# Block sums on VectorE with one operand in PSUM, and an earlier outer sum for the last output blocks, in a feed-forward kernel of 49-product matrix algebra

## The chip, the core and the metric

The kernel runs on one core of one Trainium2 chip. A core has a matrix engine (TensorE, PE in the profile, with PEld for its weight loads), VectorE (DVE), ScalarE (ACT), GpSimd (POOL), a queue engine that issues transfers (SyncE, SP), and 16 DMA engines. SBUF is the working memory, PSUM the memory into which TensorE writes. The metric is the device time in microseconds (us) of one execution.

## The reference

```python
W = cond_weights[itok]                         # one 64x64 matrix for each of 32 batch rows
y = einsum('bct,bcd->bdt', x, W)               # x: 32 x 64 x 1024
h = gelu(y @ inter_w + inter_b)                # 1024 -> 4096, tanh approximation
out = x + h @ output_w + output_b              # 4096 -> 1024
```

All is float32. The 32 x 64 rows are 2048 rows of 1024 numbers for the two large products.

## The kernel before

Each of the two large products is computed by a scheme with 7 block products in place of 8, and it is applied twice, an outer level over quarters of the matrices and an inner level inside each quarter. So each stage has 7 x 7 = 49 products per group, and sums of blocks of the operands and of the results stand around them.

**Stage one** (`mm1`, L522, tiles `fA`, `fB`, `fC`) runs `nit` = 8 iterations of 49 products. Each product is 4 matmuls of 128x256, which the trace records as 8. `OUTER` gives the order of the seven outer products, `INNER` the order of the inner seven with the PSUM tag that each uses: A, B or C, two buffers for each tag. In every block of seven, B is used by one product alone (slot 1). An outer product that completes a quarter of the hidden layer ("fin" in `hidden`) has its result read out of PSUM by VectorE, passed through Gelu on ScalarE in place, combined into sums on VectorE, and stored to DRAM as an operand of stage two. In iterations 4 to 7 (`it >= NG`) `inner_s1` also adds the second half of each Gelu result to its first half, in SBUF, one add of 128x256 (`fD<-fD` and the like in the profile) for each of the four sub-blocks "11", "21", "22" and "12".

**Stage two** (`mm3`, L533, tiles `zA`, `zB`, `zC`) runs seven outer products `o`; each has seven blocks in the order `MID`, each block seven products of 4 matmuls (8 records). `read3` reads a product out of PSUM into tiles `mX`, `mY`, `mZ`, `mD`. `mid_z` adds X to Z after block 6. After blocks 2, 7 and 3, `outer3` combines the result with that of earlier outer products, adding the bias `b2` with one instruction per 128x256 half where an output is complete (`scalar_tensor_tensor`, L934). Outputs are complete in the outer products `o` = 1, 4, 5 and 6, eight tiles in each. A complete tile is transposed by TensorE into a PSUM tile of tag "B" (t = 0) or "C" (t = 1), `add_x` adds the loaded piece of x on VectorE, and `store_out` stores it. x comes through `load_xb` into a pool of 4 buffers (`xb`), issued on SP.

Operand sums are shared: large ones on GpSimd (`pool_add`, L181), others on VectorE (`add`, also L181), for which ScalarE often copies one operand to PSUM first (`to_psum`, L198, pool `pst` of two buffers; the add then shows as `hs<-h,t`, L181). The weights' outer sums for stage two are made in stage one from pieces `w2p`, and come back through DRAM as `v`.

The order is written by hand: each step is put at a time in slots of one product (`at(time, fn)`), the steps are sorted by time, and each engine executes its instructions in that order. `base + 7.35` in `hidden` is 7.35 slots after the start of the block that completes the quarter; the next block starts at `base + 7`. A slot lasts 1.73 us, the spacing of products in the trace.

## Time and profile before

| | |
|---|---|
| median of 3 timed runs | 1388.55 us (1385.87 to 1389.38) |
| the profiled execution | 1378.28 us, of which the span of the page is 1376.5 us |
| TensorE busy | 1343.7 us (98%) |
| VectorE busy | 964.7 us (70%), 1609 instructions |
| ScalarE busy | 423.5 us (31%), 834 instructions |
| GpSimd busy | 982.1 us (71%) |
| granted TensorE clock | 0.992 of full |

The table of windows shows the stages: from 0 to 34 us the mixing of x, from 34 to 734 us stage one with TensorE busy for 695.86 of 700 us, from 734 to 1370 us stage two with 616.48 of 636 us, and then 6.5 us of tail. Times of lines below are in us from the start of the span. In a group's row the figure after the bar is its busy time in us, then the mean duration of one in ns, then the idle time of the engine just before these instructions with what ended it. In a row of the timeline the figures are start and duration in us, the square bracket is idle time before it and what ended that. Rows of the timeline merge equal neighbours (x8), and their durations overlap by some 0.2 us on TensorE.

### The profile page before, as it was taken

How to read it: one execution, taken by the hardware profiler on the slowest of the kernel's cores; microseconds unless marked ns; L12 is line 12 of the kernel's file. 1: busy time of each engine (PE TensorE's matmuls, PEld its weight loads, DVE VectorE, ACT ScalarE, POOL GpSimd, SP SyncE). 2: the span in 40 equal slices, each digit the busy share in tenths (PEclk: the TensorE clock that was granted, in tenths of full speed). 3: DMA queues.
4: the chain of work that ended last, by engine and by line, in shares of the span. 5: the costliest groups of instructions: out<-in, count | busy, mean ns of one | idle time of the engine just before them, and what ended most of it. 6: DMA issues, size and time to landing. Idle time of an engine off the chain costs nothing. (4 is left out here: it accounts for less than half of the span.)

```text
span 1376.5 us, 18801 instructions
## 1 busy us (share of the span) xinstructions
PE 1343.7 (98%) x6568; PEld 1173.6 (85%) x6568; DVE 964.7 (70%) x1609; ACT 423.5 (31%) x834; POOL 982.1 (71%) x601
## 2 busy tenths in 40 slices
PE   9999999999999999999999999989999999999897
PEld 8888888888888888888888888878888888788786
DVE  3666565575786867668667666876767677798786
ACT  3424323243352422324214312313223222231130
POOL 7754757858677594884855949949689696694791
PEclk9999999999999999999999999999999999999999
DMA  8446675878897677577757072380631806618312
GB/s 286 148 156 216 206 244 212 268 248 287 288 322 256 236 231 242 201 241 248 270 176 265 17 292 82 130 329 8 223 144 46 336 16 255 220 46 324 119 39 69
DMA packets 134942, 273.39 MB, mean 199 GB/s; under 512 B 15424, under 2 KB 67648, under 8 KB 123200
## 3 DMA queue, kind: packets, MB, share of 16 engines
q1 hardware_dynamic: 134336, 271.66, 56.6%
q8 instruction: 53, 0.87, 0.2%
q0 software_dynamic: 512, 0.53, 0.1%
q14 instruction: 41, 0.34, 0.1%
HBM read 167.28 MB, written 104.86 MB: 198 GB/s over the span
## 5 line engine op out<-in xcount | busy, mean ns | idle before, releaser
L522 PE MATMUL fA<-yi,wi 128*128 128x256 f32 x896 | 213.8, 382 | 4.1 <-DVE fD L181 2.4
L533 PE MATMUL zA<-hs,wt 128*128 128x256 f32 x840 | 200.1, 382 | 5.1 <-DVE mD L181 3.1
L181 DVE TENSOR_TENSOR hs<-h,t 128x512 f32<-128x512 f32 x308 | 199.4, 676 | 6.7 <-POOL h L181 3.5
L181 POOL TENSOR_TENSOR h<-h,h 128x1024 f32<-128x1024 f32 x84 | 203.2, 2446 | 0.0
L522 PEld LDWEIGHTS fA<-yi,wi 128*128 128x128 f32 x896 | 169.6, 190 | 31.2 <-DVE fX L181 2.8
L533 PEld LDWEIGHTS zA<-hs,wt 128*128 128x128 f32 x840 | 159.2, 192 | 28.7 <-POOL h L181 2.6
L198 ACT COPY t<-hs 128x512 f32<-128x512 f32 x112 | 66.1, 590 | 223.4 <-DVE hs L181 223.3
L181 POOL TENSOR_TENSOR wi<-w 128x512 f32<-128x512 f32 x80 | 102.9, 1286 | 29.7 <-PE fC L522 24.0
L181 POOL TENSOR_TENSOR ws<-w,w 128x1024 f32<-128x1024 f32 x32 | 76.2, 2402 | 66.8 <-PE fA L522 57.0
L547 ACT ACTIVATE fD<-fD,b 128x256 f32<-128x256 f32 x128 | 57.8, 500 | 190.3 <-DVE fD L181 190.3
L198 ACT COPY t<-h 128x512 f32<-128x512 f32 x140 | 81.3, 592 | 88.1 <-DVE hs L181 85.2
L181 DVE TENSOR_TENSOR fX<-fA,fX 128x512 f32<-128x512 f32 x104 | 71.2, 684 | 42.9 <-PE fA L522 42.5
L181 POOL TENSOR_TENSOR wt<-v 128x512 f32<-128x512 f32 x35 | 45.3, 1296 | 74.0 <-DMA v<-w_d 72.4
L181 POOL TENSOR_TENSOR wi<-w,wi 128x512 f32<-128x512 f32 x40 | 50.8, 1271 | 61.7 <-PE fA L522 54.8
L522 PE MATMUL fC<-y,wi 128*128 128x256 f32 x384 | 91.0, 380 | 0.1
L522 PEld LDWEIGHTS fC<-y,wi 128*128 128x128 f32 x384 | 72.7, 190 | 10.3 <-issue 0.5
L533 PE MATMUL zC<-hs,v 128*128 128x256 f32 x336 | 79.5, 379 | 1.3 <-ACT mX L907 1.3
L181 POOL TENSOR_TENSOR wt<-v,wt 128x512 f32<-128x512 f32 x35 | 46.4, 1326 | 46.6 <-PE zA L533 46.6
L533 PE MATMUL zA<-h,wt 128*128 128x256 f32 x336 | 79.4, 379 | 0.0
L522 PE MATMUL fA<-yi,w 128*128 128x256 f32 x320 | 75.6, 379 | 0.0
L533 PEld LDWEIGHTS zC<-hs,v 128*128 128x128 f32 x336 | 63.8, 190 | 10.3 <-ACT mX L907 1.7
L533 PEld LDWEIGHTS zA<-h,wt 128*128 128x128 f32 x336 | 63.8, 190 | 8.6
(171 smaller groups left out, 2836.7 us busy)
## 6 DMA issues: line engine op xcount, KB each, us to landing
h<-hs_d SPq DMA_DIRECT2D x56, 1024.0 KB, 6.6
w<-in_L_ffn_inter_w_dram SPq DMA_DIRECT2D x32, 1024.0 KB, 6.2
hs_d<-hs SPq DMA_DIRECT2D x96, 256.0 KB, 3.1
v<-w_d SPq DMA_DIRECT2D x21, 1024.0 KB, 9.7
hs_d<-fD SPq DMA_DIRECT2D x64, 256.0 KB, 3.4
w2p<-in_L_ffn_output_w_dram SPq DMA_DIRECT2D x32, 512.0 KB, 5.0
w_d<-w2p SPq DMA_DIRECT2D x64, 256.0 KB, 2.9
w_d<-w2t SPq DMA_DIRECT2D x48, 256.0 KB, 6.6
```

Source lines behind the costliest of these rows:

```text
L181: eng.tensor_tensor(o, a, b, ALU.subtract if sub else ALU.add)
L198: nc.scalar.copy(t, src)
L522: nc.tensor.matmul(acc[:, u, :], lt[:, k, ts(u, P)], rt[:, k, :], start=start and u == 0 and k == 0, stop=k == 1, skip_group_check=True,)
L533: nc.tensor.matmul(acc, wl[:, k, :], hr[:, k, :], start=start and k == 0, stop=k == NG - 1, skip_group_check=True,)
L547: nc.scalar.activation(t[:, u, :], t[:, u, :], AF.Gelu_apprx_tanh, bias=b1[:, f : f + 1])
```

## The change

Every sum on VectorE that had both operands in SBUF now has one of them copied to PSUM by ScalarE first.

- `to_psum` takes a tag: with one, the copy lies in a buffer of the accumulators' pool (tag "B" or "C") and not in `pst`.
- `inner_s1_copy` copies the second half of a Gelu result to a buffer of tag "B", right behind the Gelu on ScalarE; `inner_s1` adds it.
- `add_copy` replaces `mid_z`: a copy to a buffer of tag "C", and 0.6 slots later the add.
- `outer_copy` precedes `outer3` by 0.7 slots: a copy to a buffer of tag "C", or, for 2, 4 and 5, the bias added by ScalarE on the way, one instruction per half; the sum that 5 leaves carries the bias to 3. `outer3` has one add or two of 128x512 and no bias instruction.
- All transposes of outputs use tag "B".
- The last outer product: its six last pieces of x are loaded at slot 38 into two tiles of the pool `yq`, and the earlier sum X is added to Z before the last products of the last block. The last product runs in slot 7 into a buffer of tag "B" of its own, and the last tile is transposed, added and stored in halves, one of the stores on ScalarE's queue.
- The warm-up's 24 matmuls are two groups of 12 in two buffers.

```diff
+    def inner_s1_copy(it, fin, sub):
+        S1[it, fin, sub] = to_psum(H[it, fin, sub][:, 1, :], "B")
     def inner_s1(it, fin, sub):
         t = H[it, fin, sub]
-        add(nc.vector, t[:, 0, :], t[:, 0, :], t[:, 1, :])
+        add(nc.vector, t[:, 0, :], S1[it, fin, sub], t[:, 0, :])
...
             if it >= NG:
+                at(base + t + 0.01, inner_s1_copy, it, fin, subs[n])
                 at(base + t + 0.45, inner_s1, it, fin, subs[n])
...
-    def mid_z(o, t):
-        add(nc.vector, MS[o, "Z", t], MS[o, "Z", t], MS[o, "X", t])
+    def add_copy(time, dst, src):
+        e = {}
+        def one():
+            e["p"] = to_psum(src(), "C")
+        def two():
+            add(nc.vector, dst(), e["p"], dst())
+        at(time, one)
+        at(time + 0.6, two)
+    def outer_copy(o, src, blk, t):
...
+        if p in (6, 7, 3):
+            OS["p", o, blk, t] = to_psum(OS["X", blk, t] if p == 7 else m, "C")
+            return
+        ps = late["acc"].tile([P, 2, W], F32, tag="C", name=f"o{o}{blk[0]}{blk[1]}{t}")
+        n2 = STATE[p][1][1][1]
+        for n0 in range(2):
+            nc.scalar.activation(
+                ps[:, n0, :], m[:, n0, :], AF.Identity, bias=b2c(n2, blk[1], n0)
+            )
...
     def outer3(o, src, blk, t):
...
-            for n0 in range(2):
-                nc.vector.scalar_tensor_tensor(
-                    dst[:, n0, :], m[:, n0, :], b2c(STATE[p][1][1][1], blk[1], n0), y[:, n0, :],
-                    op0=ALU.add, op1=ALU.add,
-                )
+        if p == 7:
+            add(nc.vector, m, ps, m)
+        elif p == 2:
+            add(nc.vector, m, ps, x)
+        elif p == 4:
+            add(nc.vector, m, ps, v)
         else:
             if p == 5:
-                add(nc.vector, x, x, m)
+                add(nc.vector, v, ps, v)
+            add(nc.vector, x, ps, x)
...
-        tp = late["acc"].tile([P, 2, W], F32, tag="BC"[t], name=f"tp{o}_{blk[0]}{blk[1]}{t}")
+            [P, 2, W], F32, tag="B", name=f"tp{o}_{blk[0]}{blk[1]}{t}{n0s[0]}"
...
+            if (o, i) == (6, 6):
+                at(bq + 7.01, read3, o, i, (6, 7, "A", False, (1, 0)))
+                rs = INNER[:-1] + ((7, 4, "B", True, (1, 0)),)
...
-                    f = bq + (7.3, 12.4)[t] + j
-                    at(f, outer3, o, src, mb, t)
+                    f = bq + (7.1, 12.2)[t] + j
+                    if (o, i) != (6, 6):
+                        at(f, outer_copy, o, src, mb, t)
+                        at(f + 0.7, outer3, o, src, mb, t)
...
+                    at(b + 38 if (o, mb, t) in ENDS else f - 1.8, load_xb, o, mb, t)
...
+                    at(f + 2.2, transpose, o, mb, t)
+                    at(f + 3.2, add_x, o, mb, t)
+                    at(f + 4, store_out, o, mb, t)
```

More of the change, by code (lines that the diff above doesn't have):

```diff
@@ L192, with to_psum @@
     uid = [0]
-    def to_psum(src):
+    def to_psum(src, tag=None):
         uid[0] += 1
-        t = pst.tile([P, 2, W], F32, tag="t", name=f"t{uid[0]}")
-        t = t.rearrange("p k n -> p (k n)") if len(src.shape) == 2 else t
+        pool = late["acc"] if tag else pst
+        t = pool.tile([P, 2, W], F32, tag=tag or "t", name=f"t{uid[0]}")
+        if len(src.shape) == 2:
+            t = t.rearrange("p k n -> p (k n)")[:, : src.shape[1]]
         nc.scalar.copy(t, src)
@@ L279, in warm @@
         nc.vector.memset(z, 0.0)
-        t = psx.tile([P, 2, NK, D], F32, tag="py", name="warm")
-        t = t.rearrange("p j k d -> p (j k d)")
-        for _ in range(24):
-            nc.tensor.matmul(
-                t[:, :W], z[:, :P], z[:, P:], start=True, stop=True
-            )
+        for n in range(2):
+            t = psx.tile([P, 2, NK, D], F32, tag="py", name=f"warm{n}")
+            t = t.rearrange("p j k d -> p (j k d)")
+            for _ in range(12):
+                nc.tensor.matmul(
+                    t[:, :W], z[:, :P], z[:, P:], start=True, stop=True
+                )
     Y = {}
@@ L549, in gelu @@
             )
+    S1 = {}
+    def inner_s1_copy(it, fin, sub):
+        S1[it, fin, sub] = to_psum(H[it, fin, sub][:, 1, :], "B")
     def inner_s1(it, fin, sub):
         t = H[it, fin, sub]
-        add(nc.vector, t[:, 0, :], t[:, 0, :], t[:, 1, :])
+        add(nc.vector, t[:, 0, :], S1[it, fin, sub], t[:, 0, :])
     def store_h(it, fin, n):
@@ L911, in read3 @@
                 add(nc.vector, m, acc, m)
-    def mid_z(o, t):
-        add(nc.vector, MS[o, "Z", t], MS[o, "Z", t], MS[o, "X", t])
+    def add_copy(time, dst, src):
[7 more added lines that the diff above has]
+    def outer_copy(o, src, blk, t):
+        p = OUTER[o]
+        m = MS[o, src, t]
+        if p in (1, 7):
+            OS["XV"[p == 7], blk, t] = m
+        if p == 1:
+            return
+        if p in (6, 7, 3):
+            OS["p", o, blk, t] = to_psum(OS["X", blk, t] if p == 7 else m, "C")
+            return
+        ps = late["acc"].tile([P, 2, W], F32, tag="C", name=f"o{o}{blk[0]}{blk[1]}{t}")
[3 more added lines that the diff above has]
+                ps[:, n0, :], m[:, n0, :], AF.Identity, bias=b2c(n2, blk[1], n0)
+            )
+        OS["p", o, blk, t] = ps
@@ L916, in outer3 @@
     def outer3(o, src, blk, t):
         p = OUTER[o]
-        m = MS[o, src, t]
-        x = OS.get(("X", blk, t))
         if p == 1:
-            OS["X", blk, t] = m
-        elif p == 6:
-            add(nc.vector, x, x, m)
-        elif p == 7:
-            add(nc.vector, m, m, x)
-            OS["V", blk, t] = m
-        else:
-            y, dst = {
-                2: (x, m), 4: (OS.get(("V", blk, t)), m), 5: (OS.get(("V", blk, t)), "y"), 3: (x, "y"),
-            }[p]
-            dst = y if dst == "y" else dst
-            for n0 in range(2):
-                nc.vector.scalar_tensor_tensor(
-                    dst[:, n0, :], m[:, n0, :], b2c(STATE[p][1][1][1], blk[1], n0), y[:, n0, :],
-                    op0=ALU.add, op1=ALU.add,
-                )
-            OS["out", o, blk, t] = dst
-            if p == 5:
-                add(nc.vector, x, x, m)
+            return
@@ new lines, in outer3, with ends_in @@
+        m, ps = MS[o, src, t], OS["p", o, blk, t]
+        x, v = OS["X", blk, t], OS.get(("V", blk, t))
+        if p == 7:
[4 more added lines that the diff above has]
+            add(nc.vector, m, ps, v)
+        else:
+            if p == 5:
+                add(nc.vector, v, ps, v)
+            add(nc.vector, x, ps, x)
+        OS["out", o, blk, t] = {2: m, 4: m, 5: v, 3: x}.get(p)
+    def ends_in(o, blk, t):
+        OS["out", o, blk, t] = MS[o, "Z", t]
@@ L942 @@
     XB = {}
+    ENDS = [(6, mb, t) for mb in ((1, 1), (1, 0), (0, 1)) for t in range(2)]
     def place(o, blk, t):
@@ L952, in load_xb, with transpose, add_x, store_out @@
         r, c = place(o, blk, t)
-        x_t = late["xb"].tile([P, 2, W], F32, tag="xb", name=f"xb{o}_{blk[0]}{blk[1]}{t}")
+        if (o, blk, t) in ENDS:
+            k = ENDS.index((o, blk, t))
+            if k % 4 == 0:
+                XB["end", k] = yq.tile([P, 4, 2, W], F32, tag="yq", name=f"xe{k}")
+            x_t = XB["end", k - k % 4][:, k % 4]
+        else:
+            x_t = late["xb"].tile([P, 2, W], F32, tag="xb", name=f"xb{o}_{blk[0]}{blk[1]}{t}")
         nc.sync.dma_start(x_t, x_rows[r, :, c].rearrange("v p n -> p v n"))
         XB[o, blk, t] = x_t
-    def transpose(o, blk, t):
+    def transpose(o, blk, t, n0s=(0, 1)):
         d = OS["out", o, blk, t]
-        tp = late["acc"].tile([P, 2, W], F32, tag="BC"[t], name=f"tp{o}_{blk[0]}{blk[1]}{t}")
-        for n0 in range(2):
+        tp = late["acc"].tile(
+            [P, 2, W], F32, tag="B", name=f"tp{o}_{blk[0]}{blk[1]}{t}{n0s[0]}"
+        )
+        for n0 in n0s:
             for v in range(2):
                 nc.tensor.transpose(tp[:, v, ts(n0, P)], d[:, n0, ts(v, P)], late["ident"])
-        OS["tp", o, blk, t] = tp
-    def add_x(o, blk, t):
-        add(nc.vector, XB[o, blk, t], OS["tp", o, blk, t], XB[o, blk, t])
-    def store_out(o, blk, t):
+            OS["tp", o, blk, t, n0] = tp
+    def add_x(o, blk, t, n0s=(0, 1)):
+        c = slice(n0s[0] * P, (n0s[-1] + 1) * P)
+        x_t = XB[o, blk, t][:, :, c]
+        add(nc.vector, x_t, OS["tp", o, blk, t, n0s[0]][:, :, c], x_t)
+    def store_out(o, blk, t, n0s=(0, 1), eng=nc.sync):
         r, c = place(o, blk, t)
-        nc.sync.dma_start(out_rows[r, :, c].rearrange("v p n -> p v n"), XB[o, blk, t])
+        d = slice(n0s[0] * P, (n0s[-1] + 1) * P)
+        eng.dma_start(
+            out_rows[r, :, c][:, :, d].rearrange("v p n -> p v n"), XB[o, blk, t][:, :, d]
+        )
     H_LOAD = {
@@ L1004 @@
             inner_h2(bq - 2.2 if (o, i) != (0, 0) else bq + 0.7, o, q)
-            for r in INNER:
+            rs = INNER
+            if (o, i) == (6, 6):
+                at(bq + 7.01, read3, o, i, (6, 7, "A", False, (1, 0)))
+                rs = INNER[:-1] + ((7, 4, "B", True, (1, 0)),)
+            for r in rs:
                 at(bq + r[0], product3, o, i, r)
@@ L1008 @@
             if q == MID_SUM:
-                at(bq + 7.2, mid_z, o, 0)
-                at(bq + 12.2, mid_z, o, 1)
+                for t in range(2):
+                    add_copy(
+                        bq + (7.1, 12.1)[t],
+                        lambda o=o, t=t: MS[o, "Z", t], lambda o=o, t=t: MS[o, "X", t],
+                    )
             for j, (src, mb) in enumerate(MID_DONE.get(q, ())):
                 for t in range(2):
-                    f = bq + (7.3, 12.4)[t] + j
-                    at(f, outer3, o, src, mb, t)
-                    if STATE[OUTER[o]][1] is not None:
-                        at(f - 1.8, load_xb, o, mb, t)
-                        at(f + 2, transpose, o, mb, t)
-                        at(f + 3, add_x, o, mb, t)
-                        at(f + 3.8, store_out, o, mb, t)
+                    if (o, i) == (6, 6):
+                        add_copy(
+                            bq + (1.2, 4.45)[t],
+                            lambda o=o, t=t: MS[o, "Z", t],
+                            lambda mb=mb, t=t: OS["X", mb, t],
+                        )
+                        at(bq + 6.3, ends_in, o, mb, t)
+                    f = bq + (7.1, 12.2)[t] + j
+                    if (o, i) != (6, 6):
+                        at(f, outer_copy, o, src, mb, t)
+                        at(f + 0.7, outer3, o, src, mb, t)
+                    if STATE[OUTER[o]][1] is None:
+                        continue
+                    at(b + 38 if (o, mb, t) in ENDS else f - 1.8, load_xb, o, mb, t)
+                    if (o, i) == (6, 6):
+                        continue
+                    at(f + 2.2, transpose, o, mb, t)
+                    at(f + 3.2, add_x, o, mb, t)
+                    at(f + 4, store_out, o, mb, t)
+    e = end1 + 49 * 7
+    for t, n0s, time, eng in (
+        (0, (0, 1), 0.02, nc.sync), (1, (1,), 1.02, nc.scalar), (1, (0,), 2.02, nc.sync),
+    ):
+        at(e + time, transpose, 6, (0, 1), t, n0s)
+        at(e + time + 0.5, add_x, 6, (0, 1), t, n0s)
+        at(e + time + 0.6, store_out, 6, (0, 1), t, n0s, eng)
     with tc.manual_schedule():
```

## The prediction

> **What bounds the kernel now.** The page comes first. TensorE is busy for all but 2% of the span, so a gain can only come out of its few waits, out of stretches at a lower clock, and out of the tail.

> ```profile
> PE 1343.7 (98%) x6568; PEld 1173.6 (85%) x6568; DVE 964.7 (70%) x1609; ACT 423.5 (31%) x834; POOL 982.1 (71%) x601
> ```

> TensorE's own waits (columns: total us, times, longest) name VectorE in nearly every row:

> ```profile
> PE zC L533 <- DVE xb L181: 10.8, 3, 4.5
> PE zA L533 <- DVE mD L181: 3.1, 4, 1.7
> PE fA L522 <- DVE fD L181: 2.4, 1, 2.4
> ```

> Why VectorE is late there shows in the groups with shapes kept apart. One line, L934, takes 690 to 1684 ns for the same shape, by tile alone; the block sums with two SBUF operands (`fD<-fD`, `mZ<-mZ,mX`) are stretched too; sums of the same sizes with a PSUM operand are not.

> ```profile
> L181 DVE TENSOR_TENSOR hs<-h,t 128x512 f32<-128x512 f32 x308 | 199.4, 676 | 6.7 <-POOL h L181 3.5 <-ACT t L198 2.5
> ...
> L934 DVE SCALAR_TENSOR_TENSOR mD<-mD,b,mD 128x256 f32<-128x256 f32 x16 | 26.3, 1684 | 0.1
> ...
> L181 DVE TENSOR_TENSOR fD<-fD 128x256 f32<-128x256 f32 x32 | 24.6, 768 | 0.8 <-ACT fD L547 0.8
> ...
> L181 DVE TENSOR_TENSOR mZ<-mZ,mX 128x512 f32<-128x512 f32 x14 | 20.3, 1448 | 0.2
> ...
> L181 DVE TENSOR_TENSOR mX<-zA,mX 128x256 f32<-128x256 f32 x42 | 17.6, 419 | 13.6 <-PE zA L533 12.7
> ...
> L934 DVE SCALAR_TENSOR_TENSOR mY<-mY,b,mY 128x256 f32<-128x256 f32 x16 | 10.4, 690 | 0.0
> ```

> The timeline at the end of outer product 1 shows what comes of it. Two pairs of L934 take 2.96 and 2.22 us, VectorE works without a pause, and its `xb` add at 914.93 frees the PSUM buffer for which `zC` has waited 3.67 us.

> ```profile
> 904.86 2.96 DVE L934 SCALAR_TENSOR_TENSOR mX<-mX,b,mX 128x256 f32<-128x256 f32 x2
> ...
> 909.27 2.22 DVE L934 SCALAR_TENSOR_TENSOR mY<-mY,b,mY 128x256 f32<-128x256 f32 x2
> ...
> 914.93 0.68 DVE L181 TENSOR_TENSOR xb<-tp,xb 128x512 f32<-128x512 f32 x1
> ...
> 915.66 2.47 PE L533 MATMUL zC<-h,v 128*128 128x256 f32 x8 [3.67 <-DVE xb L181]
> ```

> After this wait three rows take 1.88 us more than usual (eight matmuls 2.47 against 1.89, and so on). So it is after waits of 2.41 us (at 585), 2.64 (1178) and 4.49 (1275), each time by about 1.8 us, and not after 1.75 us (1294).

> [...]

> **The change, part by part.** The sum is made against the profiled execution, 1378.28 us: the span of 1376.5 and 1.8 around it. It lies 10.3 us under the timed median; I carry the difference in us over to that.

> *VectorE's own time.* Taking 419 ns for 128x256 and 676 for 128x512: the 64 `inner_s1` save (768-419)x32 + (1038-419)x16 + (513-419)x16 = 23 us, the 14 `mid_z` 11 us, the 64 halves of L934 41 us, and the contended adds `mD<-mD,mD` (1723) and `mZ<-mZ,mZ` (1646), six each, 12 us. That is 87 us, most of it beside running matmuls, hence worth nothing by itself. ScalarE gets about 64 copies of 0.37 us, and 14 + 24 of 0.59 and 24 pairs of about 0.8: some 65 us on an engine that is 31% busy. Only the waits count.

> *Ends of outputs (three places, o = 1, 4, 5).* Waits 3.67 + 2.64 + 4.49 = 10.8, slow clock 3 x 1.8: 16.2 us now. With PSUM operands each pair of L934 becomes one add of 0.6 us (spacing in the queue), at o = 5 two. At o = 1 VectorE from 904.86 then runs nine items of 0.6 us and two of 0.34 with 0.4 of waits between them, then `xb`, done at 912.0. All transposes now share tag B, so who waits changes: not `zC`, but the second transpose ahead of it (ready at 911.33) needs that `xb`. Left is a wait of 0.7 us; counted the same way 0.2 at o = 4 and 2.0 at o = 5. Gain 16.2 - 2.9 = 13.3 us. The C copies themselves free their buffers early: the last add before `zC` ends at 908.4, and `zC` is due at 911.7.

> *Other waits of stage two.* `zA<-mD` 3.1, `zC<-mX` 1.1, `zA<-mX` 1.2 all follow a contended sum (`mZ` of 4.2 us at 1283, `mD` of 3.4 at 1212): 5.4 us. The waits for GpSimd (0.7) and ScalarE (1.3) stay.

> *Stage one, the new wait.* Each `inner_s1_copy` takes a buffer of tag B, of which there are two, and B is also a product's accumulator. By the order, the copy for "21" (slot 6.9) holds the buffer that the next block's `fB` (slot 8) takes, until `inner_s1` (7.35) has read it. So from iteration 4 on TensorE waits for VectorE at 16 places where it waited for none (15 `fB`, and the first `zB`), and all of TensorE's queue stands behind it; each chain is now Gelu, copy 0.37, add 0.42, about 0.94 us with hand-overs. The row `fV` below is "21" of the outer product before:

> ```profile
> 549.51 1.89 PE L522 MATMUL fB<-y,w 128*128 128x256 f32 x8
> ...
> 549.78 0.59 ACT L198 COPY t<-fD 128x512 f32<-128x512 f32 x1 [1.22 <-DVE fD L181]
> ...
> 550.31 1.70 ACT L547 ACTIVATE fV<-fV,b 128x256 f32<-128x256 f32 x4
> ...
> 551.24 0.42 DVE L181 TENSOR_TENSOR fV<-fV 128x256 f32<-128x256 f32 x1 [0.29 <-ACT fV L547]
> ```

> Its Gelu ends at 551.21, so `fB` could start at 552.15, not 549.51: 2.6 us late. VectorE gains some 0.3 us upstream, so I take 2.3. The same picture stands at 464 and 639. At the 13 other places, by the same reading, `fB` comes 0.8 us late at one, 0.3 at one, 0.2 at three, and has slack at the rest. Cost 3 x 2.3 + 1.7 = 8.6 us (from 3, if VectorE is ahead, to 15). Idle as the view counts it, 2.1 us, lies between 1.75 (no slow clock) and 2.41 (slow clock): 3 x 1.8 = 5.4 us, or none; I take half, 2.7. The old wait at 585 keeps most of its size: the sum falls from 1.36 to 0.42, but the copy stands ahead of it, gain 0.5.

> *The tail.* Now the last product's read, bias and transposes follow each other, and x, loaded at 1369.02 behind a store, comes last:

> ```profile
> 1368.68 0.42 DVE L181 TENSOR_TENSOR mZ<-zA,mZ 128x256 f32<-128x256 f32 x1 [0.47 <-PE zA L533]
> 1369.14 0.88 DVE L934 SCALAR_TENSOR_TENSOR mZ<-mZ,b,mZ 128x256 f32<-128x256 f32 x2
> ...
> 1372.51 0.69 DVE L181 TENSOR_TENSOR xb<-tp,xb 128x512 f32<-128x512 f32 x1 [2.49 <-issue]
> ```

> Changed: twelve transposes move behind the last product, which ends at 1366.7; then transposes and adds alternate, because two B buffers serve five tiles, and the last add ends at about 1371.1 against 1373.2. Four to five stores follow at once where there were two: gain 1.6 us (0 to 2.5). The six loads move to slot 38 on SP, behind which only stores stand, and wait for tiles of block 4 and block 6, done before slot 35: nothing. GpSimd's order does not change. The warm-up's second buffer costs nothing: it ends at 14 us, before the mixing.

> *Sum:* 13.3 + 5.4 + 0.5 + 1.6 = 20.8 saved, 8.6 + 2.7 = 11.3 lost: 9.5 us. Profiled 1368.8; median 1388.55 - 9.5 = **1379 us**.

> **The rivals.**
> - *The new wait is small (chance 0.22).* VectorE, freed of sums of 1.0 to 2.3 us, runs ahead of TensorE and `fB` finds its buffer free. For: slack of 0.7 us or more at seven of the 16. Against: at 549 the chain goes through ScalarE's queue, which the change does not relieve. Cost 2 instead of 11.3: -18.8, 1370.
> - *Nothing to measure (0.12).* ScalarE's copies put their own waits ahead of the operand copies `t<-hs`, so half of stage two's 18.7 comes back as waits for ScalarE: -0.2, 1388. That PSUM operands do not shorten a sum, the way in which the change would not do what it says, is excluded by the 308 rows of 676 ns.
> - *Slower (0.15).* The wait of `fB` for `inner_s1` decides: at all 16 places VectorE and ScalarE are as late as at 549. 16 x 2.1 = 33.6, less 20.8: +13, 1401, more with a slow clock. It decides from a mean of 1.3 us over the 16. Against it: the slack above.

> **How the numbers follow.** The forecast has 0.51, its own range 1371 to 1386 (the fB cost 3 to 15, slow clock 0 to 5.4, tail 0 to 2.5). The whole range, 1369 to 1391, takes in nearly all of the small-wait case and the no-change case and leaves out most of the slower one. About 0.3% (4.2 us) is what a measurement of this kernel tells from no change: faster 0.73 (the forecast nearly whole, the first rival), same 0.13, slower 0.14.

> **What would show it.** Right: sums at 419 and 676 ns with no spread; `zC<-xb` gone from TensorE's waits, a transpose waiting for `xb` for under 2 us; new rows of `fB` waiting for VectorE's `fV`, near 464, 549 and 639, of about 2 us; `xb` adds for the last tile without a wait for x. Wrong: `fB` rows of under 3 us in total (rival one) or over 20 (the slower one), or rows of TensorE waiting for ScalarE in stage two (the second).

## The result and the profile after

| | before | after |
|---|---|---|
| timed median (6 runs each, side by side) | 1390.39 us (1385.87 to 1392.29) | 1380.47 us (1377.36 to 1380.68) |
| profiled execution | 1378.28 us | 1380.57 us |
| span and mean clock of it | 1376.5 us, 0.992 | 1378.8 us, 0.985 |
| VectorE, ScalarE busy | 964.7, 423.5 us | 883.4, 487.5 us |

The ratio of the timed runs is 0.9927 (95% interval 0.9909 to 0.9945): the change makes the kernel 10 us faster. The two profiled executions, put side by side without a second thought, say that it got 2 us slower. So the first thing to do with this pair is to find out why.

Here is the first section of the page of after, busy time by engine:

```profile
PE 1353.6 (98%) x6568; PEld 1184.9 (86%) x6568; DVE 883.4 (64%) x1579; ACT 487.5 (35%) x984; POOL 961.4 (70%) x601
```

VectorE lost 81 us and ScalarE gained 64. TensorE's busy time went up by 10 us for the same 6568 matmuls, so somewhere its matmuls were slower. The windows of the two profiles show where (columns: stretch, length, TensorE busy with its matmuls, granted clock, DMA share, GB/s). Of before, 20 to 50 us:

```profile
20.00:30.00 10.00, 10.00 (x184) 1.00 1.09 347
30.00:50.00 20.00, 18.13 (x99) 0.83 0.38 109
```

and of after:

```profile
20.00:30.00 10.00, 10.00 (x98) 0.50 1.01 350
30.00:50.00 20.00, 20.00 (x179) 0.50 0.13 5
```

In after, the mixing of x runs at half clock from 20 us to its end near 48 us (98 matmuls between 20 and 30 us where before has 184). Nothing of the change stands there but the warm-up's second buffer. Whether that start belongs to the change or to the execution is the first experiment's question.

TensorE's waits in after (total us, times, longest):

```profile
PE fB L525 <- DVE fV L181: 7.9, 4, 2.5
PE tp L1006 <- DVE xb L181: 3.1, 3, 2.2
...
PE fA L525 <- DVE fD L181: 0.8, 1, 0.8
```

Of the rows of before, `zC` waiting for `xb` (10.8) and `zA` waiting for `mD` (3.1) are gone. New are `fB` waiting for `fV` (and once, 0.7 us, for `fD`, which is the same kind of wait), and transposes waiting for `xb`. For ScalarE TensorE waits once, 1.3 us (`zC` for `mX`), as in before.

The groups with shapes kept apart show sums of one length for one shape. The mean in ns (behind the busy time) has lost its spread; `t` and `o` are the copies in PSUM:

```profile
L181 DVE TENSOR_TENSOR fD<-t,fD 128x256 f32<-128x256 f32 x32 | 13.3, 415 | 2.7 <-ACT t L200 2.7
...
L181 DVE TENSOR_TENSOR mD<-o,mD 128x512 f32<-128x512 f32 x8 | 5.3, 685 | 1.6 <-ACT o L949 1.6
...
L181 DVE TENSOR_TENSOR mZ<-t,mZ 128x512 f32<-128x512 f32 x20 | 13.7, 685 | 0.5
```

The `fD` sums took 768 ns and take 415; a block of `mD` took two instructions of 1684 and takes one of 685; `mZ` took 1448 and takes 685. The bias (L949) costs ScalarE 477 ns per half.

The timeline of after, first at the end of outer product 1 (the place shown at 915.66 for before), then at the end of outer product 5:

```profile
932.16 0.68 DVE L181 TENSOR_TENSOR xb<-tp,xb 128x512 f32<-128x512 f32 x1
...
932.89 0.66 PE L1006 MATMUL tp<-ident,mY 128*128 128x128 f32 x4 [0.42 <-DVE xb L181]
933.39 1.89 PE L536 MATMUL zC<-h,v 128*128 128x256 f32 x8
...
1281.66 0.66 PE L1006 MATMUL tp<-ident,mY 128*128 128x128 f32 x4 [2.21 <-DVE xb L181]
1282.16 3.12 PE L536 MATMUL zC<-h,v 128*128 128x256 f32 x8
```

At product 1 the transpose waits 0.42 us where `zC` waited 3.67, and `zC` behind it takes 1.89 us, not 2.47. At product 5 the transpose still waits 2.21 us, with low clock behind it (3.12 us for eight matmuls in place of 1.89). And this is the new wait of stage one:

```profile
569.14 0.38 ACT L200 COPY t<-fV 128x256 f32<-128x256 f32 x1
...
569.55 0.42 DVE L181 TENSOR_TENSOR fV<-t,fV 128x256 f32<-128x256 f32 x1 [0.70 <-ACT t L200]
...
570.03 1.99 PE L525 MATMUL fB<-y,w 128*128 128x256 f32 x8 [2.46 <-DVE fV L181]
```

Gelu, copy, add, and 0.06 us after the add's end `fB` starts: it takes the buffer that the copy held. The same stands at 480.77 (2.45) and 659.75 (2.46).

### The profile page after: what moved, and what is told of

The parts are those of the page before. It is cut to its first block, busy times and chain, and to the rows that moved or that the text cites. A ratio compares the mean times of both kernels' runs of the same rounds, so it can differ in the third digit from the quotient of the medians.

```text
span 1378.8 us, 18997 instructions
## 1 busy us (share of the span) xinstructions
PE 1353.6 (98%) x6568; PEld 1184.9 (86%) x6568; DVE 883.4 (64%) x1579; ACT 487.5 (35%) x984; POOL 961.4 (70%) x601
## 4 chain that ended last, share of the span: by engine, by line
PE 92%; DVE 4%; ACT 1%; issue 1%; DMA 1%; POOL 0%; DVEq 0%; ACTq 0%
PE fA L525 26%; PE zA L536 23%; PE fC L525 13%; PE zC L536 12%; PE fB L525 7%; PE zB L536 6%; PE py L308 2%; DVE hs L181 1%; PE tp L1006 1%; PE warm L286 1%; PE pl L308 1%; ACT t L200 1%; DMA y<-y_d 1%; DVE fX L181 1%; DVE fV L181 1%
## 5 line engine op out<-in xcount | busy, mean ns | idle before, releaser
L181 DVE TENSOR_TENSOR hs<-h,t 128x512 f32<-128x512 f32 x308 | 199.8, 678 | 7.1 <-ACT t L200 3.4
L181 POOL TENSOR_TENSOR h<-h,h 128x1024 f32<-128x1024 f32 x84 | 196.1, 2361 | 0.6 <-DMA h<-hs_d 0.6
L181 POOL TENSOR_TENSOR ws<-w,w 128x1024 f32<-128x1024 f32 x32 | 74.8, 2360 | 75.2 <-PE fA L525 75.1
L181 POOL TENSOR_TENSOR wi<-w 128x512 f32<-128x512 f32 x80 | 101.7, 1271 | 30.5 <-PE fC L525 24.6
L181 POOL TENSOR_TENSOR wt<-v 128x512 f32<-128x512 f32 x35 | 44.5, 1272 | 82.2 <-DMA v<-w_d 78.4
L181 DVE TENSOR_TENSOR fX<-fA,fX 128x512 f32<-128x512 f32 x104 | 71.3, 685 | 47.0 <-PE fA L525 46.7
L181 POOL TENSOR_TENSOR wi<-w,wi 128x512 f32<-128x512 f32 x40 | 50.8, 1271 | 61.7 <-PE fA L525 55.0
L525 PEld LDWEIGHTS fC<-y,wi 128*128 128x128 f32 x384 | 72.7, 190 | 10.4 <-issue 0.5
L536 PEld LDWEIGHTS zC<-hs,v 128*128 128x128 f32 x336 | 63.8, 190 | 10.3 <-ACT mX L916 1.7
L525 PE MATMUL fB<-y,w 128*128 128x256 f32 x256 | 63.6, 393 | 7.9 <-DVE fV L181 7.9
## 6 DMA issues: line engine op xcount, KB each, us to landing
v<-w_d SPq DMA_DIRECT2D x21, 1024.0 KB, 10.8
```

Of the source, the lines that this page charges most:

```text
L181: eng.tensor_tensor(o, a, b, ALU.subtract if sub else ALU.add)
L525: nc.tensor.matmul(acc[:, u, :], lt[:, k, ts(u, P)], rt[:, k, :], start=start and u == 0 and k == 0, stop=k == 1, skip_group_check=True,)
L536: nc.tensor.matmul(acc, wl[:, k, :], hr[:, k, :], start=start and k == 0, stop=k == NG - 1, skip_group_check=True,)
```

## The experiments

Each kernel was timed beside before on one chip; ratios are to before, with 95% intervals. There were three sessions (runs 1 to 4; 5 to 8; 9 and 10), in which before had medians of 1391.6, 1391.6 and 1391.0 us; differences to after are taken to its 1380.47 us of the first measurement. "Version n" is the kernel of run n.

**1. The kernel before, unchanged, profiled again.** No edit.

> The kernel before, unchanged, for a second profile. Theory A (the start): the profile of before shows a start that its timed runs did not have. In the timed runs TensorE's clock falls to half during the mixing of x, as it does in the profile of after (0.5 from about 20 to 53 us), and that is the 10 us between the profiled 1378.28 and the median 1388.6. Then this profile has a span near 1387, a mean clock of 0.985 to 0.987 and the first fA near 43 us, where the first profile has it at 33.97; from there on both agree to 1 us. Theory B: the 10 us are spread over both stages (longer waits for VectorE); then the first fA starts near 34 again and the rows of TensorE's waits are longer than 10.8, 3.1 and 2.4.

Measured: 1391.60 us, ratio 0.9999 (0.9989 to 1.0008); its profiled execution took 1392.02 us, span 1390.2, clock 0.981. Its windows, and its timeline at the start:

```profile
20.00:30.00 10.00, 10.00 (x104) 0.53 0.99 341
30.00:50.00 20.00, 20.00 (x177) 0.50 0.14 8
```

```profile
18.45 0.21 PE L305 MATMUL py<-wsel_e,x 64*128 64x64 f32 x1 [1.09 <-issue]
19.16 15.49 PE L305 MATMUL py<-wsel_e,x 64*128 64x64 f32 x154 [0.50 <-issue]
...
48.44 3.36 PE L522 MATMUL fA<-y,w 128*128 128x256 f32 x8
```

The half clock belongs to the kernel before as well, not to the change. TensorE has three pauses between 16 and 19 us that the profile puts down to "issue", then mixes at half clock, and the first `fA` starts at 48.44 us; in the first profile of before the pauses are missing and it starts at 33.97. Of the 20 timed runs of this kernel none has a mean clock above 0.984; the first profile, at 0.992, caught a start that is rare. (That trace has its own stretch at half clock, from 33.0 to 39.8 us.) Theory A holds; that stages one and two otherwise agree to 1 us does not quite: the waits for `xb` come to 12.1 us here against 10.8, and low clock differs from place to place (behind the same wait of 3.67 us eight matmuls of `zC` take 3.78 us here and 2.47 in the first profile).

From here on, after is compared with this profile. The span is cut at the starts of two matmuls that both programs have: the last ahead of the first `pl`, and the last ahead of stage two's first wait of `zC` for `mX`.

| stretch | before, second profile | after | difference |
|---|---|---|---|
| start to the first cut | 68.69 us | 70.05 us | +1.4 |
| first to second cut (stage one) | 685.18 | 694.29 | +9.1 |
| second cut to the end (stage two) | 636.30 | 614.46 | -21.8 |
| span | 1390.17 | 1378.80 | -11.4 |

**2. After, with the stage-one part undone.**

```diff
-                at(base + t + 0.01, inner_s1_copy, it, fin, subs[n])
...
-        add(nc.vector, t[:, 0, :], S1[it, fin, sub], t[:, 0, :])
+        add(nc.vector, t[:, 0, :], t[:, 0, :], t[:, 1, :])
```

> After, with the stage-one part undone: inner_s1 adds two SBUF operands as before, no copies in tag B. Theory A (the new wait is real and all of it is lost): the fB rows that wait for fV (7.9 us in the profile of after, and 1.7 of low clock behind the first) go away; the wait near 585 to 600 comes back (2.6 + 1.8 in before, 1.1 now), so 1380.5 - 9.6 + 3.3 = 1374. Theory B (VectorE's 23 us freed in stage one are worth something beside the wait): the plain sums make other waits longer, 1380 or more.

Measured: 1372.92 us, ratio 0.9869 (0.9853 to 0.9885), 7.6 us under after. The `fB` rows are gone, and `fA` waits for `fD` for 2.4 us again:

```profile
PE fA L525 <- DVE fD L181: 2.4, 1, 2.4
```

Between the cuts of the table, stage one takes 685.24 us in this trace, as in before (685.18). Theory A holds: stage two and the tail bring 18.7 us against before in the timed runs, and the stage-one part takes 7.6 of them back.

**3. After, with one copy of four left out.**

```diff
+                if n != "21":
                     at(base + t + 0.01, inner_s1_copy, it, fin, subs[n])
...
-        add(nc.vector, t[:, 0, :], S1[it, fin, sub], t[:, 0, :])
+        add(nc.vector, t[:, 0, :], S1.get((it, fin, sub), t[:, 1, :]), t[:, 0, :])
```

> After, with one of the four copies of each quarter left out: the sum for 21 adds two SBUF operands as before, the other three keep their copy in tag B. Theory A: only the copy for 21 meets fB, so the fB rows go (9.6 us with the low clock) and nothing comes back: 1371, and faster than the version with the whole stage-one part undone by 3 us. Theory B: the buffer of another copy (22, one slot later) is then the one that fB waits for, or the longer sum of 21 delays the operands behind it: 1376 to 1380.

Measured: 1369.83 us, ratio 0.9844 (0.9830 to 0.9857), 10.6 us under after. Of TensorE's waits in this kernel the longest for a sum of stage one:

```profile
PE fA L525 <- DVE fD L181: 1.3, 1, 1.3
```

No row of `fB` is left, and the wait of `fA` is 1.3 us where version 2, without any copy, has 2.4. So the whole loss sat in the copy for "21", the one whose buffer the next block's `fB` takes. The other three are worth 3.1 us (1372.92 to 1369.83).

**4. After, with the old warm-up.**

```diff
-        for n in range(2):
-            t = psx.tile([P, 2, NK, D], F32, tag="py", name=f"warm{n}")
...
-            for _ in range(12):
+        t = psx.tile([P, 2, NK, D], F32, tag="py", name="warm")
...
+        for _ in range(24):
```

> After, with the old warm-up: 24 matmuls into one buffer. Theory A: the second buffer of the warm-up is worth nothing, 1380.5 within 1 us, and the mixing of x runs at half clock as in after. Theory B: the two groups of the warm-up are what lets the mixing begin or keeps TensorE from its pause near 17 us: the start changes by some us in one direction (first fA not near 48), and the time with it.

Measured: 1380.47 us, ratio 0.9916 (0.9902 to 0.9930), clock 0.985: no difference. The warm-up's second buffer is worth nothing. In effect the run is also a second measurement of after, in another session, with the same median.

**5. Before, with all transposes in tag B.**

```diff
-        tp = late["acc"].tile([P, 2, W], F32, tag="BC"[t], ...
+        tp = late["acc"].tile([P, 2, W], F32, tag="B", ...
```

> Before, with all transposes of outputs in tag B (one part of the change alone); VectorE's sums stay as they were. Theory A (the gain of stage two comes from VectorE being on time, not from which buffer is waited for): the second transpose now waits for the same xb add at the same moment, so the waits of 3.7, 2.6 and 4.5 us stay under another name: 1391.6 within 1.5 us. Theory B (the gain came from taking the transposes out of tag C, so that zC is free): the three waits go with their low clock, 16 us, 1375 to 1378.

Measured: 1394.76 us, ratio 1.0021 (1.0014 to 1.0029): slower by 3 us, outside Theory A's 1.5, and on the other side from Theory B. Its waits:

```profile
PE tp L962 <- DVE xb L181: 12.8, 4, 5.6
```

The wait of `zC` has only changed its name. The gain of stage two therefore does not come from the buffer. What the 3 us are is not settled: in the trace one wait of `zA` for `mD` has grown from 1.8 to 3.1 us, but that profiled execution was the fastest of this kernel (1389.83 us).

**6. After, with the last output ended as before.**

```diff
-    ENDS = [(6, mb, t) for mb in ((1, 1), (1, 0), (0, 1)) for t in range(2)]
+    ENDS = []
+    LAST = None
...
-            if (o, i) == (6, 6):
+            if (o, i) == LAST:
...
-    e = end1 + 49 * 7
-    for t, n0s, time, eng in (
...
```

> After, with the end of the last output as before (x loaded late in slots of its own, transposes ahead of the last product, no halves, no store on ScalarE), but with the sums from PSUM. Theory A: the tail is worth 1.6 us (0 to 2.5): 1382.1. Theory B: with VectorE on time the old tail loses its waits too and is as good: 1380.5 within 0.5. Theory C: the old tail's late load of x (it waited for a store) now decides alone: 1384 or more.

Measured: 1380.29 us, ratio 0.9920 (0.9904 to 0.9936). Theory B holds: the new tail is worth nothing. The timelines say why. After (last product, last add; span 1378.8):

```profile
1368.74 1.89 PE L536 MATMUL zB<-h,wt 128*128 128x256 f32 x8
...
1373.98 1.02 DVE L181 TENSOR_TENSOR xe<-tp,xe 128x512 f32<-128x512 f32 x2 [0.42 <-PE tp L1006]
```

and this kernel (span 1378.98):

```profile
1370.46 1.89 PE L536 MATMUL zA<-h,wt 128*128 128x256 f32 x8
...
1374.97 0.69 DVE L181 TENSOR_TENSOR xb<-tp,xb 128x512 f32<-128x512 f32 x1 [0.81 <-PE tp L1007]
```

In after the last product ends at 1370.63 and the last add at 1375.00, 4.4 us later; with the old tail the ends are 1372.35 and 1375.66, 3.3 us apart. The product comes 1.7 us sooner in these two executions, the adds behind it take 1.1 us longer, and the last stores 0.5 (3.8 us from the last add to the end against 3.3). In before that first distance was 4.2 us (1382.66 to 1386.84 in the second profile), because the last `xb` add waited for x; with the sums on time it does not.

**7. Version 3 with full-size matmuls in the mixing.** Twelve calls, which the profile shows as 24 matmuls; the results are overwritten.

```diff
             out = [py[:, j] for j in range(2)]
+            if i in FIRST and FIRST.index(i) in (2,):
+                w = py.rearrange("p j k d -> p (j k d)")
+                for _ in range(12):
+                    nc.tensor.matmul(
+                        w[:, :W], XT[i][:, :P], XT[i][:, P : 3 * P], start=True, stop=True
+                    )
```

> The version with only the copy for 21 left out (1369.8), and ahead of the third tile of the mixing of x 12 matmuls of 128x128x256 whose result is overwritten. Theory A (the half clock from 20 to 50 us holds because the mixing's 64x64 matmuls do not bring the clock back, and full-size matmuls do, as the first fA rows show each time): the 12 take about 5 us, then the clock is 1 and the remaining 256 matmuls take 14 us and not 28: first fA near 40 and not 49.4, 1360 to 1362. Theory B (the clock is held down by something else in that stretch, the loads for one, or the pause for instructions comes back as soon as the matmuls are fast): the 12 only add their time or the pause takes the gain: 1370 to 1375.

Measured: 1362.46 us, ratio 0.9790 (0.9773 to 0.9807), 7.4 us under version 3, clock 0.997. The windows:

```profile
20.00:30.00 10.00, 10.00 (x51) 0.68 0.94 342
30.00:50.00 20.00, 18.30 (x272) 1.00 0.28 55
```

The 24 matmuls run from 22.0 to 29.6 us, the clock is full from about 26.5 us on (its mean from 25 to 30 us is 0.85, from 30 us on 1.00), and the first `fA` starts at 44.0 us. Theory A, a little short of its numbers (40 us and 1360 to 1362 were expected): the 12 calls took 7.6 us and not 5, and `fB` then waits 1.7 us for the mixed x. The loads are not what holds the clock down, since it comes back while they go on (394 GB/s from 25 to 30 us). The pauses at 16 to 19 us stay; what "issue" hides there was not tried.

**8. Version 3 with the add of x earlier in VectorE's queue.**

```diff
-                    at(f + 3.2, add_x, o, mb, t)
+                    at(f + 2.5, add_x, o, mb, t)
```

> The version with only the copy for 21 left out (1369.8), and VectorE's add of x (add_x) 0.7 slots earlier in its queue, ahead of two sums at outer product 5. Theory A (the 2.2 us that a transpose still waits for xb at the end of outer product 5, with 1.7 us of low clock behind it, is a matter of the place in VectorE's queue): the wait falls to about 0.9 and the low clock goes, 1366 to 1367. Theory B (VectorE's sums for GpSimd and TensorE that now stand behind the xb add are late in turn, or VectorE stands waiting for the transpose): the same wait under another name, 1369 to 1371.

Measured: 1366.27 us, ratio 0.9816 (0.9798 to 0.9834), 3.6 us under version 3. At the end of outer product 5:

```profile
1268.00 0.68 DVE L181 TENSOR_TENSOR xb<-tp,xb 128x512 f32<-128x512 f32 x1
...
1268.74 0.66 PE L1007 MATMUL tp<-ident,mY 128*128 128x128 f32 x4 [0.43 <-DVE xb L181]
```

The wait of 2.21 us is 0.43 (0.9 expected), the two of 0.42 us are gone, and no other row grew by more than 0.2 us. It was a matter of the place in the queue.

**9. After, with stage two's new adds reading SBUF twice.** The bias is added in place by ScalarE; the copies are left out.

```diff
-            e["p"] = to_psum(src(), "C")
+            e["p"] = src()
...
-            OS["p", o, blk, t] = to_psum(OS["X", blk, t] if p == 7 else m, "C")
+            OS["p", o, blk, t] = OS["X", blk, t] if p == 7 else m
...
-        ps = late["acc"].tile([P, 2, W], F32, tag="C", name=f"o{o}{blk[0]}{blk[1]}{t}")
+        ps = m
```

> After, with stage two's new adds taking both operands from SBUF: ScalarE puts the bias into the block in place (two instructions per block, as in after), the copies in tag C are left out, and VectorE's one add per block and mid_z read SBUF twice. Instructions on VectorE are as many as in after. Theory A (the PSUM operand is what counts): the adds of 128x512 take 0.7 to 2.3 us again where GpSimd works, VectorE is late at the ends of outputs 1, 4 and 5, and roughly half of stage two's 20.8 us goes: 1386 to 1391. Theory B (the bias moved to ScalarE, one add for two L934, is what counts): the rows of TensorE waiting for xb stay near 3 us, 1380 to 1383.

Measured: 1385.63 us (1380.95 to 1389.81), ratio 0.9963 (0.9951 to 0.9976): 5.2 us over after, between the theories and nearer to A. One group and one wait of it, from the fastest of its executions:

```profile
L181 DVE TENSOR_TENSOR mD<-mD,mD 128x512 f32<-128x512 f32 x14 | 22.1, 1587 | 0.5 <-ACT mD L949 0.4
```

```profile
PE tp L1006 <- DVE xb L181: 6.4, 3, 4.3
```

With two SBUF operands the sums are stretched again, and the longest wait for `xb` is 4.3 us where after has 2.2. But a block of `mD` takes one sum of 1.59 us, where before took two of 1.68. So the PSUM operand is worth 5.2 us of stage two. What is left is the bias on ScalarE, which halves VectorE's instructions per block where an output is complete: 13.5 us, if 5.2 is taken from the 18.7 of the timed runs, and 18.4 by the traces, where stage two takes 617.89 us between the same cuts and 636.30 in before. That is a subtraction, and the rest of stage two's edits is in it; the bias was not moved alone, so that it carries the larger part is argued and not shown.

**10. Version 3 with both, 7 and 8.** The edits are those two.

> The three gains together: copy for 21 left out, 12 full-size matmuls ahead of the third tile of the mixing, add_x 0.7 slots earlier. If they are independent: 1369.8 - 7.4 - 3.6 = 1358.9, within 1 us, which is 2.3% under before. If one of them only shifts a wait into another's place: 1361 or more.

Measured: 1359.35 us (1358.56 to 1360.10), ratio 0.9772 (0.9755 to 0.9789). The three gains add up (1358.9 expected). This is the fastest version here, 21 us under after. TensorE does 24 matmuls more than in after and is busy for 13 us less (1340.4 us against 1353.6), since fewer of them run at half clock (mean clock 0.998 against 0.985).

## Why the prediction was right, and where its steps were off

The forecast said 9.5 us saved and 1379 us; measured are 9.9 us and 1380.47. Between the spans of the second profile of before and of after the saving is 11.4 us. Step by step:

| step | forecast | measured |
|---|---|---|
| VectorE's own time | -87 us | -81.3 us (964.7 to 883.4) |
| ScalarE's | +65 us | +63.9 us |
| waits for `xb` left at outputs 1, 4, 5 | 0.7, 0.2, 2.0 us | 0.42, 0.42, 2.21 us, and 1.7 of low clock behind the last |
| stage two and tail together | -20.3 us | -21.8 us in the traces, -18.7 in the timed runs |
| new waits of `fB` | 8.6 us, three of 2.3 | 8.6 us (7.9 for `fV`, 0.7 for `fD`), three of 2.46 |
| low clock behind them | 2.7 us | 1.7 us, behind one of the three |
| stage one as a whole | +10.8 us | +9.1 us in the traces, 7.6 in the timed runs |
| tail | -1.6 us | -0.2 us by the spans, +0.2 by the medians |

- **The new wait** was found in the order of the program and sized by a Gelu, a copy and an add in the trace of before: 0.94 us from the Gelu's end was forecast, 0.92 measured (569.11 to 570.03). The rival in which VectorE runs ahead and `fB` finds its buffer free is excluded by the row of 7.9 us; the slower one, in which all 16 places are late, by the count of five waits; and the one in which half of stage two's gain comes back as waits for ScalarE by the single wait of 1.3 us, which before has too.
- **Who waits at the ends of outputs** was right too: not `zC` but the second transpose, and the wait left at output 5 was in the forecast (2.0 us). The low clock behind it was not: the sum charges half a fall of the clock to each `fB` wait of 2.1 us and none to this one, which had one in after.
- **The reason given for stage two was too simple.** The prediction put the shorter sums down to the PSUM operand and the single add together. The run that takes away the PSUM operand alone loses only 5.2 us; by subtraction, halving the number of instructions carries most. The long sums themselves are, in the trace of before, sums beside GpSimd: of its 166 sums with two SBUF operands the 68 with no GpSimd instruction alongside took 407 to 426 ns (128x256), 471 to 485 (L934) and 677 to 682 (128x512), while of the 98 with one alongside 80 took over 10% longer, up to 2837 ns. The step "each pair of L934 becomes one add of 0.6 us" was right for both together, which is why the sum came out.
- **The tail** is the mis-sized term: 1.6 us forecast, nothing measured. The step compared the new tail with the old one as the trace of before shows it, with its late VectorE and its wait for x. With the sums on time the old tail ends as early. A part of a change has to be priced in the kernel that the other parts leave.
- **The low clock** was not worked out but halved: 5.4 us or none for the three waits of `fB`, and 2.7 was taken. One of the three had it in after, the one at 480.77 us (eight matmuls at 622 ns each); in version 6 the same wait did not (392 ns). That the sum came within 0.4 us of the measured saving is luck in part: the tail's 1.6 us and the low clock at output 5 were missed, and stage one came out cheaper than forecast.
- **The difference of 10.3 us between profile and median** was carried over without knowing what it was. It turned out to be the half clock during the mixing, which the traces of after, of version 3 and of before taken again have (0.50 from 30 to 50 us) and the first one of before has not. The forecast held because the change does not touch it; had it touched the start, the sum would have been made against the wrong one.

## What to carry to other kernels

A copy to PSUM that shortens a sum takes a buffer, and the price is paid by whoever takes that buffer next: ask for every copy which instruction comes next in that tag, and whether the buffer can still be held when that is due. Here three of four copies were worth 3 us together, and the fourth cost 10.6. Where a profiled execution is shorter than the median, find the stretch that differs before you build on it; here the windows of a second profile showed it, and the repair of that stretch was worth 7.4 us, three quarters of what the whole change brought. And a wait of TensorE can cost more than its own length: of the five waits of 2.21 to 2.46 us in before and after, three cost some 1.7 us more in low clock and two nothing. Version 8 shortened one such wait from 2.21 to 0.43 us and two of 0.42 to nothing, 2.6 us in all, and was 3.6 us faster than version 3.

## What the runs showed of the hardware that was not expected

```profile
477.13:480.54 3.41, 1.19 (x6) 1.00 0.68 259
480.54:483.95 3.41, 3.18 (x8) 0.50 0.95 329
...
565.87:569.28 3.41, 1.70 (x8) 1.00 0.91 338
569.28:572.69 3.41, 2.66 (x12) 1.00 1.01 351
...
654.62:658.03 3.41, 2.67 (x13) 1.00 0.86 274
658.03:661.44 3.41, 1.69 (x8) 1.00 0.99 347
```

The first wait leaves 2.22 us idle in one stretch (3.41 less 1.19), and the next stretch is at half clock. The other two, of the same length, are cut in two by the end of a stretch (1.71 and 0.75 us, 0.74 and 1.72), and the clock stays. In the two traces together, from the first `fA` to the last matmul, all six stretches at full clock with 2.03 us of idle time or more (2.41, 2.03, 2.09 and 3.10 us in before, 2.22 and 2.21 in after) were followed by half clock, and none of the 765 others, of which the idlest has 1.75 us. So in these traces it is not the length of a wait that tells, but how much of it falls into one stretch; the waits of 2.64, 3.67 and 4.49 us had 2.09, 2.03 and 3.10 us in one. The eight stretches at half clock with 0.23 us of idle time or less were each the last of their kind; the one from 32.99 us in before, with 0.98 us, was followed by another. At half clock a busy TensorE loses half of such a stretch, which is the 1.7 us found behind most of these waits (at 480.77 in after eight matmuls take 3.55 us in place of 1.89). During the mixing less idle time was followed by a fall as well: 0.89 us in the stretch that ends at 32.99 us in before, and in after 1.75 us in the stretch from 16.32 us, which holds the pauses. Why it differs there was not shown.
- **The time of before scatters more (1387 to 1395 us) than that of version 3 (1369.5 to 1370.3).** Version 3 has one wait of over 1.9 us once the start is over (2.2 us); before has four. The first trace of before has four low stretches behind these waits. The mean clocks of its timed runs, 0.979 to 0.984 in the session of run 1, would fit a number of low stretches that changes from run to run, one being worth 0.001 of the mean (half of 3.41 us in 1390). This is the author's estimate: timed runs have no trace to show it.
